# Second cross-attention of a two-layer decoder: a step's stages in another order, and the maxima of two heads turned together

## The chip, the cores and the metric

The kernel runs on one core of a Trainium2 chip, in float32. The metric is the device time of one execution in microseconds. Four runs of the kernel before gave 878.8 to 882.66, with a median of 880.27.

## The reference

A decoder of two layers works on `x` (8 sequences of 128 tokens, 256 wide) and a context `ctx_2048` of the same shape. Each layer is self-attention, cross-attention and a feed-forward part, each added to its input and followed by a layernorm. The last feed-forward part is a mixture of 64 experts with 8 chosen per token. The part that matters here is the cross-attention of the second layer; query is `x`, key and value are the context, both taken "as they lie" and cut into heads by reshaping:

```python
b, d, m = q.shape                  # 8, 128, 256
qh = q.reshape(b * h, d // h, m)   # h = 8 heads of 16 rows
kh = k.reshape(b * h, d // h, -1)
vh = v.reshape(b * h, c // h, -1)
qk = jnp.einsum('bdm,bdn->bmn', qh, kh) * scale
sm = jax.nn.softmax(qk, axis=-1)
ret = jnp.einsum('bmn,bcn->bcm', sm, vh)
```

A head is thus 16 of the 128 token rows, and its attention runs over the 256 columns. After it comes `x = _layernorm(x + ret)`, and then the routing of the experts: logits `x @ gate_w.T`, their softmax, the top 8 of 64.

## The kernel before

The parts of the decoder follow each other; within a part, work is cut into units and run as a pipeline written in Python and fully unrolled. On PE the order of instructions is the order in which the program issues them (`manual_schedule` for the tensor engine). On DVE, ACT and POOL a planner fixes the order when the kernel is built, by its own costs and by when it takes an operand to be ready; the program's order is its priority among ready instructions. The planner also gives out the buffers.

The second cross-attention works on 16 units (b, par): sequence b, and par 0 or 1 for one of the two heads in each block of 32 rows. So a unit has four heads, in row blocks j = 0 to 3 at rows 32j. It runs in these stages:

- `limits` (L803) copies the query on POOL with only the rows of this par kept (L806), and computes scores for maxima on PE (L812): four matmuls of 32 rows into four PSUM tiles `y_s`, each 128 query columns by 2 x 256 keys, both pars at once, for the half c = par of the query columns. Then DVE takes the four maxima, negated (L820, "maxima").
- `shift` (L824) turns the maxima on PE (L827, two transposes into one PSUM tile `y_m`), so that each lands in a spare row beside its head's query rows, and adds the query on DVE (L829). A row of ones in the keys then subtracts the maximum within the scores' matmul.
- `weights` (L832) computes transposed scores (L836, four PSUM tiles `y_sT`), and ACT their exponentials (L843, "y_e").
- `weigh` (L848) multiplies by the values and by ones for the sums (L855). For par 1 it ends the sequence: a reciprocal and a product on DVE (L862, L864), an addition on POOL (L866, on DVE for the last sequence), and a layernorm over DVE and POOL (L181 to L192).
- `turn_x`, `choose` and `place` (L869, L887, L912) do the routing for two sequences at a time (one at a time for the last two): a DMA of the rows to memory (L876) and transposes on PE (L880), the gate's matmuls and the top 8 on DVE (L894 to L909), then the places within the experts (L924 to L930) and the softmax (L944 to L951).

The pool `ps_x` has six PSUM buffers of one bank. From it come the tiles of `limits` (four), of `weights` (four), of `shift` (one) and of the routing (one each). The two sums of `weigh` lie in another pool of two.

`run_pipelined` (L44) runs one unit further at each step; within a step it goes through the stages from the deepest to the first, so that a step before issues: `place` of unit s-8, `choose` s-7, `turn_x` s-6, `weigh` s-4, `weights` s-3, `shift` s-2, `limits` s. After each of the first three steps `finish_heads` (L957) issues a sequence of the self-attention's output projection. There are 24 steps, 0 to 23; the last `limits` is in step 15, the last `weigh` in step 19.

Of the kernel before, what the change touches and what calls it, by code (L numbers as in the profile page):

```python
# [9 lines left out]
F32 = mybir.dt.float32  # L10
# [4 lines left out]
ALU = mybir.AluOpType  # L15
AX = mybir.AxisListType

P = 128
B = 8
# [24 lines left out]
def run_pipelined(units, stages, between=lambda step: None):  # L44

    states = [{} for _ in units]
    for step in range(len(units) + len(stages) - 1):
        for depth in range(len(stages) - 1, -1, -1):
            n = step - depth
            if 0 <= n < len(units):  # L50
                stages[depth](states[n], *units[n])
        between(step)
# [7 lines left out]
def decoder_kernel(ctx: ExitStack, tc: tile.TileContext, i, out):  # L60
    nc = tc.nc
# [33 lines left out]
    ident = cp.tile([P, P], F32, name="ident")  # L95
# [14 lines left out]
    rows_of, quarter = [], []  # L110
    for par in range(2):
        m = cp.tile([P, 1], F32, name=f"rows_{par}")
# [3 lines left out]
        q = cp.tile([P, 1], F32, name=f"quarter_{par}")  # L116
# [5 lines left out]
    def load(name, shape, src, dtype=F32, pool=cp):  # L122
        t = pool.tile(shape, dtype, name=name)
        nc.sync.dma_start(out=t, in_=src)
        return t
# [7 lines left out]
    for h in range(HALVES):  # L133
        t = xtp.tile([P, 2, HT], F32, tag="xT", name=f"xT0_{h}")
# [6 lines left out]
    for p in range(PAIRS):  # L141
        t = xsp.tile([P, 2, D], F32, tag="xs", name=f"x0_{p}")
# [19 lines left out]
    cx = load("cx", [P, B, D], i["ctx"].rearrange("b s d -> s b d"))  # L162
# [319 lines left out]
    with l0, tc.tile_pool(name="l0a", bufs=2) as ap:  # L482
# [33 lines left out]
        held = {}  # L516
# [139 lines left out]
    keys = kpool.tile([P, B, 2, D], F32, name="keys")  # L656
# [3 lines left out]
    one_row = []  # L660
    for par in range(2):
        m = cp.tile([P, 1], F32, name=f"one_row_{par}")
        nc.vector.reduce_sum(m, one_at[:, 1 - par, 0, :], axis=AX.X)
        one_row.append(m)
        t = cp.tile([P, 1], F32, name=f"kept_{par}")
# [3 lines left out]
    def make_constants():  # L669

        nc.gpsimd.memset(before, 1.0)
        nc.gpsimd.affine_select(
            before, before, pattern=[[1, P]], compare_op=ALU.is_gt, fill=0.0, base=0, channel_multiplier=-1
        )
        nc.gpsimd.iota(iota, pattern=[[1, P]], base=0, channel_multiplier=0, allow_small_or_imprecise_dtypes=True)
        nc.gpsimd.iota(starts, pattern=[[P, P]], base=0, channel_multiplier=0, allow_small_or_imprecise_dtypes=True)
        nc.gpsimd.iota(
            numbers, pattern=[[S, B]], base=0, channel_multiplier=1, allow_small_or_imprecise_dtypes=True
        )
        nc.gpsimd.tensor_scalar(numbers, numbers, 1.0 / (B * S), 1.0, ALU.mult, ALU.add)  # L680
        nc.gpsimd.iota(turns, pattern=[[1, TOP]], base=0, channel_multiplier=0, allow_small_or_imprecise_dtypes=True)
        nc.gpsimd.iota(rows_16, pattern=[[1, P], [0, TOP]], base=0, channel_multiplier=0, allow_small_or_imprecise_dtypes=True)
        nc.gpsimd.tensor_scalar(rows_16, rows_16, -MIDDLE, None, ALU.add)
        nc.gpsimd.iota(blks_16, pattern=[[1, NG], [0, TOP]], base=0, channel_multiplier=0, allow_small_or_imprecise_dtypes=True)
        nc.gpsimd.memset(seen[:, 0, :], 0.0)
        for par in range(2):
            nc.gpsimd.tensor_scalar(keys[:, :, par, :], cx, quarter[par], one_row[par], ALU.mult, ALU.add)

# [81 lines left out]
    def ps_x(name):  # L772
        return psx.tile([P, 512], F32, tag="x", name=name)

    with (
# [6 lines left out]
        cxT = load("cxT", [P, 2, B, S], i["ctxT"].rearrange("(k p) b c -> p k b c", p=P), pool=ap)  # L782
        values, sums_w, maxima = [], [], []
        for n in range(2):
            t = ap.tile([P, 2, 2, P], F32, name=f"maxima_{n}")
            nc.gpsimd.memset(t.rearrange("p a c r -> p (a c r)"), 0.0)
            maxima.append(t)
        for par in range(2):
            t = ap.tile([P, 2 * B, 4, 2, 16], F32, name=f"values_{par}")
            nc.gpsimd.memset(t.rearrange("p a j two r -> p (a j two r)"), 0.0)  # L790
            nc.gpsimd.tensor_copy(
                t[:, :, :, par, :],
                cxT.rearrange("p k b (j two r) -> p (k b) j two r", two=2, r=16)[:, :, :, par, :],
            )
            values.append(t.rearrange("p (k b) j two r -> p k b (j two r)", k=2))
            t = ap.tile([P, 2, 16], F32, name=f"sums_w_{par}")
            nc.gpsimd.memset(t[:, 1 - par, :], 0.0)
            nc.gpsimd.memset(t[:, par, :], 1.0)
            sums_w.append(t.rearrange("p two r -> p (two r)"))
        def rows_at(j):  # L800
            return slice(32 * j, 32 * j + 32)

        def limits(st, b, par):  # L803

            q = xp.tile([P, D], F32, tag=f"qm{par}", bufs=3, name=f"y_qm_{b}_{par}")
            nc.gpsimd.tensor_scalar(q, x4[b // 2][:, b % 2, :], kept[par], None, ALU.mult)  # L806
            st["q"] = q

            c = par
            tiles = [ps_x(f"y_s_{b}_{c}_{j}").rearrange("p (par n) -> p par n", par=2) for j in range(4)]  # L810
            for j in range(4):
                nc.tensor.matmul(  # L812
                    tiles[j], x4[b // 2][rows_at(j), b % 2, c * P : (c + 1) * P], keys[rows_at(j), b],
                    start=True, stop=True,
                )
            flat = maxima[b % 2].rearrange("p par c r -> p (par c r)")
            for j in range(4):

                at = c * P + 32 * j + 16
                nc.vector.tensor_reduce(  # L820
                    flat[:, at : at + 2 * P - 15 : 2 * P - 16], tiles[j], AX.X, ALU.max, negate=True
                )

        def shift(st, b, par):  # L824
            pt = ps_x(f"y_m_{b}_{par}")[:, : 2 * P]
            for c in range(2):
                nc.tensor.transpose(pt[:, c * P : (c + 1) * P], maxima[b % 2][:, par, c, :], ident)  # L827
            t = xp.tile([P, D], F32, tag=f"qs{par}", name=f"y_q_{b}_{par}")
            nc.vector.tensor_tensor(t, pt, st["q"], ALU.add)  # L829
            st["q"] = t  # L830

        def weights(st, b, par):  # L832
            tiles = [ps_x(f"y_sT_{b}_{par}_{j}").rearrange("p (k m) -> p k m", k=2) for j in range(4)]
            for k in range(2):
                for j in range(4):
                    nc.tensor.matmul(  # L836
                        tiles[j][:, k, :], keys[rows_at(j), b, par, k * P : (k + 1) * P], st["q"][rows_at(j), :],
                        start=True, stop=True,
                    )
            st["e"] = []  # L840
            for j in range(4):
                e = xp.tile([P, 2, D], F32, tag="ye", bufs=8, name=f"y_e_{b}_{par}_{j}")
                nc.scalar.activation(e, tiles[j], AF.Exp)  # L843
                st["e"].append(e)

        held = {}

        def weigh(st, b, par):  # L848
            if par == 0:
# [18 lines left out]

        def turn_x(st, b, par):  # L869

            st["seqs"] = {(1, 1): (0, 2), (3, 1): (2, 2), (5, 1): (4, 2), (7, 0): (6, 1), (7, 1): (7, 1)}.get((b, par))
            if st["seqs"] is None:
                return
            b0, n = st["seqs"]
            x = x5[b0 // 2][:, b0 % 2 : b0 % 2 + n, :]
            nc.sync.dma_start(out=xd[b0 * S : (b0 + n) * S, :].rearrange("(b s) d -> s b d", s=S), in_=x)  # L876
            pt = ps_x(f"pt_moe_{b0}")[:, : 2 * n * S].rearrange("p (k t) -> p k t", k=2)
            for k in range(2):
                for bb in range(n):
                    nc.tensor.transpose(  # L880
                        pt[:, k, bb * S : (bb + 1) * S], x[:, bb, k * P : (k + 1) * P], ident
                    )
            t = xp.tile([P, 2, 2 * S], F32, tag="xT_moe", name=f"xT_moe_{b0}")
            nc.scalar.copy(t[:, :, : n * S], pt)
            st["xT"] = t
# [71 lines left out]
        def finish_heads(step):  # L957

            b = B // 2 + 1 + step
            if b < B:  # L960
                add_heads(b, 0, L1_HEADS)
                if b == B - 1:
                    l1v.close()

        run_pipelined(
            [(b, par) for b in range(B) for par in range(2)],
            [limits, idle, shift, weights, weigh, idle, turn_x, choose, place],
            finish_heads,
        )

    keys_pool.close()
    open_banks()
# [250 lines left out]
    for b in range(B):  # L1223
# [8 lines left out]
        r = tp.tile([P, D], F32, tag="r", bufs=4, name=f"moe_r_{b}")  # L1232
        nc.vector.tensor_tensor(r, ps, acc, ALU.add)
        st = sm.tile([P, 6], F32, tag="ln_st", name=f"st_l1f_{b}")
# [5 lines left out]
        shift = sm.tile([P, 1], F32, tag="ln_shift", name=f"shift_l1f_{b}")  # L1240
# [66 lines left out]
```

## Time and profile before

| what | value |
|---|---|
| median of four runs | 880.27 us |
| the profiled execution | 880.5 us, span of the trace 878.6 us |
| scores for maxima, first to last start (L812) | 466.3 to 580.2 us |
| transposed scores (L836), first to last start | 492.7 to 595.1 us |
| end of the last `weigh` on PE | 600.1 us |
| routing and the first gathers | to 631 us |
| experts and output | to 878.6 us |
| PE busy over the span | 806.3 us (92%) |
| DVE, ACT, POOL busy | 460.3, 287.9, 231.7 us |
| DVE busy from 510.06 to 522.25 | 8.84 of 12.19 us |
| ACT busy in the same stretch | 4.13 us |

The span is the time from the first to the last instruction in the trace of one execution. A row of the timeline gives the start and the length of a group of like instructions, the engine, the line, what is written from what, their number, and in brackets the idle time before it with what ended it. PE rows are matmuls; PEld rows are the loading of a matmul's weights, which overlaps them. In the table of windows a row gives a stretch of time, its length, the busy time of PE, PEld, DVE, ACT and POOL (with the number of instructions), the clock granted to PE as a share of full speed, the share of the DMA engines and their GB/s.

### The profile page before, as it was taken

The numbers are of one execution on the slowest core, as the hardware profiler recorded it, in microseconds if no ns is written. First come the engines' busy times: TensorE is split into PE (matmuls) and PEld (weight loads), VectorE is DVE, ScalarE is ACT, GpSimd is POOL, SyncE is SP. The second block draws the span as 40 slices with busy tenths as digits, with TensorE's granted clock in tenths as the row PEclk, the third lists the DMA queues.
The fourth block names the chain that finished last, engine by engine and source line by source line (L and its number), as shares of the span: only waits on it lengthen the run. The fifth ranks groups of instructions, "written<-read, shape, count | busy, mean of one in ns | idle before, by whom it ended". The sixth has DMA issues, their size and how long they took to land. (4 is left out here: it accounts for less than half of the span.)

```text
span 878.6 us, 14286 instructions
## 1 busy us (share of the span) xinstructions
PE 806.3 (92%) x4588; PEld 541.1 (62%) x4588; DVE 460.3 (52%) x1280; ACT 287.9 (33%) x990; POOL 231.7 (26%) x321
## 2 busy tenths in 40 slices
PE   8899988999999999999999999995689888999946
PEld 5455643666455558555557655553578878888835
DVE  2799885314544432344444576756795333343326
ACT  2577751221333330233340132332332332333302
POOL 0011122216100001000014131111566655555524
PEclk9999996999999999999999998987599999999969
DMA  5400011920000000000010000000678887988665
GB/s 184 141 1 1 2 49 49 309 74 1 0 1 0 1 1 1 0 1 1 1 43 6 1 14 1 13 13 13 210 228 284 284 279 235 299 288 293 208 238 232
DMA packets 39730, 87.80 MB, mean 100 GB/s; under 512 B 6432, under 2 KB 16192, under 8 KB 38752
## 3 DMA queue, kind: packets, MB, share of 16 engines
q1 hardware_dynamic: 32352, 68.96, 23.8%
q0 software_dynamic: 6144, 16.79, 5.6%
q10 hardware_dynamic: 1152, 1.05, 0.4%
q8 instruction: 41, 0.67, 0.3%
q14 instruction: 41, 0.34, 0.1%
HBM read 76.29 MB, written 10.49 MB: 99 GB/s over the span
## 5 line engine op out<-in xcount | busy, mean ns | idle before, releaser
L224 ACT ACTIVATE l_e<-l_s,nm_l 128x128 f32<-128x128 f32 x256 | 90.2, 369 | 91.6 <-DVE nm_l L221 91.2
L1142 PE MATMUL moe_gu_few<-cols,w_few 128*128 (+1 forms) x832 | 114.9, 282 | 4.8 <-DVE cols L1121 1.9
L1142 PEld LDWEIGHTS moe_gu_few<-cols,w_few 128*128 128x128 f32 x832 | 103.0, 195 | 11.7 <-issue 8.9
L1172 POOL DMA_INDIRECT pair_rows<-moe_os_few,pairs x64 | 63.1, 986 | 54.0 <-DVE moe_os_few L1171 37.8
L1096 POOL DMA_INDIRECT xg_few<-x_rows,tok_i x60 | 62.0, 1034 | 32.2 <-PE moe_gu_few L1142 12.9
L1159 PE MATMUL moe_o_few<-moe_h_few,w_few 128*128 128x128 f32 x416 | 63.9, 277 | 0.0
L740 PE MATMUL l_q<-xT_l1a,w_qkv 128*128 128x512 f32 x128 | 60.2, 593 | 0.0
L843 ACT ACTIVATE y_e<-y_sT 128x512 f32<-128x512 f32 x64 | 33.0, 604 | 83.0 <-PE y_sT L836 50.3
L740 PE MATMUL l_v<-xT_l1a,w_qkv 128*128 128x512 f32 x128 | 60.1, 592 | 0.0
L740 PE MATMUL l_k<-xT_l1a,w_qkv 128*128 128x512 f32 x128 | 60.1, 592 | 0.0
L1162 ACT COPY cols<-moe_o_few 128x256 f32 (+1 forms) x104 | 38.8, 373 | 62.7 <-PE moe_oT_few L1169 22.3
L231 DVE TENSOR_SCALAR l_e<-l_e,inv_l 128x128 f32<-128x128 f32 x256 | 58.3, 292 | 1.4
L723 DVE TENSOR_TENSOR l_vs<-l_c,l_vs 128x512 f32<-128x512 f32 x32 | 22.1, 692 | 67.4 <-PE l_c L722 67.4
L703 PE MATMUL l_y<-w_o,l_vs 128*128 128x256 f32 x256 | 56.9, 381 | 0.0
L1159 PEld LDWEIGHTS moe_o_few<-moe_h_few,w_few 128*128 128x128 f32 x416 | 55.2, 193 | 0.0
L703 PEld LDWEIGHTS l_y<-w_o,l_vs 128*128 128x128 f32 x256 | 48.1, 190 | 9.9 <-issue 2.8
L1150 ACT ACTIVATE moe_s_few<-moe_gu_few 128x128 f32<-128x128 f32 x104 | 29.0, 279 | 76.3 <-PE moe_gu_few L1142 45.9
L224 ACT ACTIVATION_READ_ACCUMULATOR l_e<-l_s,nm_l 128x1 f32 x256 | 53.1, 207 | 0.0
L1121 DVE COPY cols<-moe_xT_few 128x256 f32<-128x256 f32 x64 | 26.5, 418 | 47.0 <-PE moe_o_few L1159 22.7
L1152 DVE TENSOR_TENSOR moe_h_few<-moe_gu_few,moe_s_few 128x128 f32<-128x128 f32 x104 | 29.8, 287 | 40.2 <-ACT moe_s_few L1150 25.5
L221 DVE TENSOR_REDUCE nm_l<-l_s 128x4 f32<-128x512 f32 x64 | 43.2, 685 | 10.0 <-PE l_s L755 8.1
L748 ACT COPY l_vs<-l_v 128x512 f32<-128x512 f32 x32 | 18.7, 585 | 78.6 <-PE l_v L740 78.6
(267 smaller groups left out, 1360.7 us busy)
## 6 DMA issues: line engine op xcount, KB each, us to landing
w_few<-in_experts SPq DMA_DIRECT2D x104, 384.0 KB
z<-pair_rows SPq DMA_DIRECT2D x7, 1024.0 KB
w_qkv<-in_w_qkv SPq DMA_DIRECT2D x8, 768.0 KB
w_o<-in_w_o SPq DMA_DIRECT2D x1, 2048.0 KB
xT<-in_xT SPq DMA_DIRECT2D x2, 512.0 KB
x<-in_x SPq DMA_DIRECT2D x4, 256.0 KB
cx<-in_ctx SPq DMA_DIRECT2D x1, 1024.0 KB
q_up<-in_up_qT SPq DMA_DIRECT2D x4, 256.0 KB
```

Source lines behind the costliest of these rows:

```text
L221: nc.vector.tensor_reduce(nm, s, AX.X, ALU.max, negate=True)
L224: nc.scalar.activation(e[:, a, :], s[:, a, :], AF.Exp, bias=nm[:, a : a + 1], scale=1.0, accum_out=sums[:, a : a + 1],)
L231: nc.vector.tensor_scalar(e[:, a, :], e[:, a, :], inv[:, a : a + 1], None, ALU.mult)
L703: nc.tensor.matmul(py[:, :D], scaled[b // 4, m][:, b % 4 * S : (b % 4 + 1) * S], w_o[:, m, :], start=(m == 0), stop=(m == L1_HEADS - 1),)
L740: nc.tensor.matmul(ps, w_qkv[:, k, c, n, :], xT[h][:, k, :], start=(k == 0), stop=(k == 1))
L843: nc.scalar.activation(e, tiles[j], AF.Exp)
L1096: nc.gpsimd.indirect_dma_start(out=x, out_offset=None, in_=xd, in_offset=bass.IndirectOffsetOnAxis(ap=tok_i[:, g : g + 1], axis=0), bounds ...
L1142: mm = nc.tensor.matmul(ps[:, a, :], ws[v][:, at : at + P], cols[:, k, bass.ds(o + P, P)], start=(k == 0), stop=(k == 1),)
L1152: nc.vector.tensor_tensor(hid, ps[:, 1, :], s, ALU.mult)
L1159: nc.tensor.matmul(ps[:, c, :], ws[v][:, at : at + P], hs[v], start=True, stop=True)
L1162: cp = nc.scalar.copy(cols[:, :, bass.ds(o, P)], ps)
L1172: inst = nc.gpsimd.indirect_dma_start(out=zd, out_offset=bass.IndirectOffsetOnAxis(ap=pairs[:, g : g + 1], axis=0), in_=o, in_offset=None, ...
```

## The change

Three things change together.

The order within a step is written out: `weights`, `weigh`, `place`, `choose`, `turn_x`, `shift`, `limits`, at the same depths 3, 4, 8, 7, 6, 2, 0 as before, in the same 24 steps.

The maxima of both pars are kept in one tile of half the width, with the place for a par 0 head's maximum at 32j + 16 of its block and for a par 1 head's at 32j. `shift` turns this tile once for a sequence, at par 0, and holds the PSUM tile for par 1. The DVE instruction now multiplies the turned tile by a mask of one row per block (`one_row`) and adds the query, so that each par sees its own maximum alone. The halves of the keys change places so that this fits.

The routing of the first three pairs of sequences starts at units (2, 0), (4, 0) and (6, 0) and so one step later; that of the last two sequences is unchanged.

```diff
-            nc.gpsimd.tensor_scalar(keys[:, :, par, :], cx, quarter[par], one_row[par], ALU.mult, ALU.add)
+            nc.gpsimd.tensor_scalar(keys[:, :, 1 - par, :], cx, quarter[par], one_row[par], ALU.mult, ALU.add)
...
-            t = ap.tile([P, 2, 2, P], F32, name=f"maxima_{n}")
+            t = ap.tile([P, 2, P], F32, name=f"maxima_{n}")
...
-                at = c * P + 32 * j + 16
-                nc.vector.tensor_reduce(
-                    flat[:, at : at + 2 * P - 15 : 2 * P - 16], tiles[j], AX.X, ALU.max, negate=True
-                )
+                at = c * P + 32 * j
+                nc.vector.tensor_reduce(flat[:, at : at + 17 : 16], tiles[j], AX.X, ALU.max, negate=True)
...
         def shift(st, b, par):
-            pt = ps_x(f"y_m_{b}_{par}")[:, : 2 * P]
-            for c in range(2):
-                nc.tensor.transpose(pt[:, c * P : (c + 1) * P], maxima[b % 2][:, par, c, :], ident)
+
+            if par == 0:
+                held[b, "m"] = ps_x(f"y_m_{b}")[:, : 2 * P]
+                for c in range(2):
+                    nc.tensor.transpose(held[b, "m"][:, c * P : (c + 1) * P], maxima[b % 2][:, c, :], ident)
             t = xp.tile([P, D], F32, tag=f"qs{par}", name=f"y_q_{b}_{par}")
-            nc.vector.tensor_tensor(t, pt, st["q"], ALU.add)
+            nc.vector.scalar_tensor_tensor(t, held[b, "m"], one_row[par], st["q"], ALU.mult, ALU.add)
...
-                        tiles[j][:, k, :], keys[rows_at(j), b, par, k * P : (k + 1) * P], st["q"][rows_at(j), :],
+                        tiles[j][:, k, :], keys[rows_at(j), b, 1 - par, k * P : (k + 1) * P], st["q"][rows_at(j), :],
...
-            st["seqs"] = {(1, 1): (0, 2), (3, 1): (2, 2), (5, 1): (4, 2), (7, 0): (6, 1), (7, 1): (7, 1)}.get((b, par))
+            st["seqs"] = {(2, 0): (0, 2), (4, 0): (2, 2), (6, 0): (4, 2), (7, 0): (6, 1), (7, 1): (7, 1)}.get((b, par))
...
-        run_pipelined(
-            [(b, par) for b in range(B) for par in range(2)],
-            [limits, idle, shift, weights, weigh, idle, turn_x, choose, place],
-            finish_heads,
-        )
+        units = [(b, par) for b in range(B) for par in range(2)]
+        states = [{} for _ in units]
+        stages = [(weights, 3), (weigh, 4), (place, 8), (choose, 7), (turn_x, 6), (shift, 2), (limits, 0)]
+        for step in range(len(units) + 8):
+            for stage, depth in stages:
+                if 0 <= step - depth < len(units):
+                    stage(states[step - depth], *units[step - depth])
+            finish_heads(step)
```

More of the change, by code (lines that the diff above doesn't have):

```diff
@@ L784, in decoder_kernel @@
         for n in range(2):
-            t = ap.tile([P, 2, 2, P], F32, name=f"maxima_{n}")
-            nc.gpsimd.memset(t.rearrange("p a c r -> p (a c r)"), 0.0)
+            t = ap.tile([P, 2, P], F32, name=f"maxima_{n}")
+            nc.gpsimd.memset(t.rearrange("p c r -> p (c r)"), 0.0)
             maxima.append(t)
@@ L799, in decoder_kernel @@
             sums_w.append(t.rearrange("p two r -> p (two r)"))
+        held = {}
         def rows_at(j):
@@ L815, in limits @@
                 )
-            flat = maxima[b % 2].rearrange("p par c r -> p (par c r)")
+            flat = maxima[b % 2].rearrange("p c r -> p (c r)")
             for j in range(4):
-                at = c * P + 32 * j + 16
-                nc.vector.tensor_reduce(
-                    flat[:, at : at + 2 * P - 15 : 2 * P - 16], tiles[j], AX.X, ALU.max, negate=True
-                )
+                at = c * P + 32 * j
+                nc.vector.tensor_reduce(flat[:, at : at + 17 : 16], tiles[j], AX.X, ALU.max, negate=True)
         def shift(st, b, par):
-            pt = ps_x(f"y_m_{b}_{par}")[:, : 2 * P]
-            for c in range(2):
-                nc.tensor.transpose(pt[:, c * P : (c + 1) * P], maxima[b % 2][:, par, c, :], ident)
+            if par == 0:
+                held[b, "m"] = ps_x(f"y_m_{b}")[:, : 2 * P]
+                for c in range(2):
+                    nc.tensor.transpose(held[b, "m"][:, c * P : (c + 1) * P], maxima[b % 2][:, c, :], ident)
             t = xp.tile([P, D], F32, tag=f"qs{par}", name=f"y_q_{b}_{par}")
-            nc.vector.tensor_tensor(t, pt, st["q"], ALU.add)
+            nc.vector.scalar_tensor_tensor(t, held[b, "m"], one_row[par], st["q"], ALU.mult, ALU.add)
             st["q"] = t
@@ L844, in weights @@
                 st["e"].append(e)
-        held = {}
         def weigh(st, b, par):
```

## The prediction

> **What bounds the kernel now.** I read the page first, then the PE timeline of the second cross-attention, then DVE's, then a table of windows for the clock. The page's second part has slices of 22 us; the changed step fills slices 21 to 27.
>
> ```profile
> PE   8899988999999999999999999995689888999946
> PEclk9999996999999999999999998987599999999969
> ```
>
> PE is above 90% busy there, and its granted clock dips in slices 24 and 26. So the step is PE's, but "busy" hides waits inside a group: a group's length against its shortest one shows them. One pair of steps in PE's timeline (start, length, line; the PEld rows are weight loads, with the wait in brackets):
>
> ```profile
> 516.48 1.15 PE L836 MATMUL y_sT<-y_q,keys 32*128 32x256 f32 x16
> 517.92 2.53 PE L812 MATMUL y_s<-keys,x 32*128 32x512 f32 x8
> 518.84 0.29 PEld L812 LDWEIGHTS y_s<-keys,x 32*128 32x128 f32 x2 [0.20 <-ACT y_e L843]
> 519.33 0.29 PEld L812 LDWEIGHTS y_s<-keys,x 32*128 32x128 f32 x2 [0.20 <-ACT y_e L843]
> 522.25 2.21 PE L836 MATMUL y_sT<-y_q,keys 32*128 32x256 f32 x16
> 523.33 0.72 PEld L836 LDWEIGHTS y_sT<-y_q,keys 32*128 32x128 f32 x10 [0.30 <-DVE maxima L820]
> 524.78 2.10 PE L812 MATMUL y_s<-keys,x 32*128 32x512 f32 x8
> ```
>
> The scores for maxima (L812) take 1.08 us where nothing holds them (484.57 to 485.65) and 2.1 to 2.5 here: their third and fourth tile wait for an exponential to give back a PSUM buffer. The scores (L836) take 1.08 alone and 2.1 where the maxima on DVE hold the buffers. Six buffers serve two groups of four, so whichever group comes right behind the other waits for the engine that empties the first. From 510.06 to 522.25 is 12.19 us for a pair of steps; PE's own work in it is 2 x (1.08 + 1.87 + 1.08 + 0.36) = 8.8. The weighing, 1.87 (514.62 to 516.48), lies between maxima scores and scores and covers DVE. DVE in those microseconds:
>
> ```profile
> 516.62 1.76 DVE L862 RECIPROCAL y_inv<-y_z 128x256 f32<-128x256 f32 x1 [0.39 <-PE y_z L855]
> 519.68 0.43 DVE L187 BATCH_NORM_STATS2 st_l1x<-y_r 128x6 f32<-128x256 f32 x1 [0.84 <-POOL y_r L866]
> 521.33 0.41 DVE L192 TENSOR_SCALAR x<-y_r,mv_l1x,rs_l1x 128x256 f32<-128x256 f32 x1 [1.00 <-POOL rs_l1x L182]
> 521.99 2.48 DVE L820 TENSOR_REDUCE maxima<-y_s 128x2 f32<-128x512 f32 x4
> ```
>
> Behind each second weighing stands a reciprocal and a layernorm, 5.1 us with two waits for POOL; the four maxima take 0.62 each. The clock, in windows cut at its own changes (behind each stretch its length, then busy time and instructions of PE, PEld, DVE, ACT and POOL, then the granted clock):
>
> ```profile
> 532.64:536.06 3.42, 3.42 (x43) 1.91 (x40) 2.38 (x7) 0.00 (x0) 1.73 (x3) 1.00 0.02 5
> 536.06:539.47 3.41, 2.56 (x23) 1.50 (x20) 3.17 (x15) 1.18 (x6) 0.00 (x0) 0.99 0.01 2
> 539.47:542.88 3.41, 3.41 (x10) 1.85 (x8) 2.50 (x7) 1.47 (x4) 0.92 (x1) 0.50 0.00 0
> 594.08:597.50 3.42, 2.67 (x25) 1.52 (x24) 2.78 (x16) 2.02 (x7) 0.00 (x0) 1.00 0.13 43
> ```
>
> A stretch of 3.41 us with 2.56 busy is followed by 6.8 us at half clock (twice, after 536 and 567, where the maxima scores wait for the routing's buffer); one with 2.67 is not.
>
> **The change, part by part.** I call a step odd where the weighing ends a sequence and the reciprocal follows. In the new order a step issues scores, weighing, (routing), turning, maxima scores. The exponentials now have the weighing as cover: scores end at 1.08, the fourth exponential about 1.2 + 2.06 = 3.3 us after their start (516.48 to 519.76), the maxima scores begin at 2.95 at the earliest and need their last buffer later: that wait goes. But maxima scores and the next scores are now neighbours, and what is late next is DVE.
>
> *Even step.* Weighing 1.87, turning 0.36, maxima scores. The first maximum starts 1.16 behind them (524.78 to 525.94); the scores' third tile needs the first, the fourth the second: 1.16 + 2 x 0.62 + 0.1 = 2.5, and 1.05 from the last release to the next group (523.33 to 524.38). 1.87 + 0.36 + 3.55 = 5.78. The turning used to lie in the exponentials' shadow and cost nothing; halved in number it now stands in the open.
>
> *Odd step.* DVE's order is fixed at build time, and the trace of before does not show it for this neighbourhood. Counted from the weighing's start: weighing to 1.87, reciprocal 2.01 to 3.77. With one maximum put between reciprocal and product, and one behind it: 4.39, product 4.81, second maximum 5.43, +0.1 + 1.05 = 6.58. Bounds: two maxima ahead of the product, 6.16; one behind the product and one behind the statistics, 7.45; all behind the layernorm (2.01 + 5.12 + 1.24 + 1.15), 9.5. I take 6.58, because of the tail of before:
>
> ```profile
> 600.13 1.76 DVE L862 RECIPROCAL y_inv<-y_z 128x256 f32<-128x256 f32 x1 [3.04 <-PE y_z L855]
> 601.81 0.17 DVE L901 MAX8 r_top<-gate 128x8 f32<-128x64 f32 x1
> 601.93 0.42 DVE L864 TENSOR_TENSOR y_r<-y_av,y_inv 128x256 f32<-128x256 f32 x1
> ```
>
> There a ready instruction was put between reciprocal and product. A pair is 12.36, against 12.19: an even trade.
>
> *Small edits.* The shift becomes a SCALAR_TENSOR_TENSOR; between its 0.29 (128x128, L930) and 0.69 (128x512, L935) lies 0.42 for 128x256, what L829 takes now. If the second shift were put late, the turned tile would hold a sixth buffer and the even steps wait for a third maximum: 6 x 0.62 = 3.7 more; zero taken. Smaller memsets and swapped halves of the keys on POOL: nothing, they lie under the first layer's heads. The three early DMAs of x rows go to SP's queue a step later; behind them there only the expert weights wait, first issued at 618.3.
>
> *Routing.* On PE the same 0.6 + 1.1 + 1.14 per block. But the top-8 choice now falls into odd steps (11 and 15): 1.8 + 0.65 us of DVE work (537.16 to 538.95 and the combine) join the reciprocal's; POOL's gaps take about 0.9, 1.5 remain on the path, twice 3.0. PE then idles some 1.5 us behind its first tile, so each keeps its clock loss. Price of one: between 2.2 (a routing block of four steps takes 30.3, two plain pairs and routing 27.2, less 0.85 idle) and 3.4 (half of 6.83); I take 2.8.
>
> *Plain odd steps.* Two tiles hold PE to about 3.8 (an estimate from the 1.05 that a tile's two halves take), the third starts at 4.5, the fourth at 5.53: 0.9 idle, 2.5 of 3.41 busy, under the 2.56 that cost the clock. The stretch from 3.8 to 5.53 lies whole in one window with a chance of (3.41 - 1.73)/3.41, about a half; of four plain odd steps two: 5.6.
>
> *Tail.* From the end of the scores of unit 13 to the last weighing's end: 585.18 to 600.03, 14.85, before, since each weighing waits for its exponentials. After: four weighings 7.48, two scores 2.16, placing 1.1, turning 0.36 and 0.7 for its shift, transposes 0.6: 12.4. Behind it, the choice of sequences 4 and 5 now falls into the last layernorm: 2.45 less DVE's 0.57 idle there, 1.9.
>
> *Sum.* The first scores start at 492.75 as before; those of unit 1 end at 498.0 (3.9 + 1.08 + 0.3). Six pairs 74.2, routing 4.5, choice 3.0, two clock losses 5.6: 585.3. Tail 12.4, choice 1.9: 599.6, against 600.03. Two more clock losses: +5.2. Routing, experts and output follow unchanged. The span of 878.6 belongs to a run of 880.5, the median is 880.27: **885.5**.
>
> **A page against the rows.** The Trainium skill, "TensorE: Matmul & The Clock Gate", section "Why this matters for your kernels", allows idle gaps up to about 3 us; by it the changed kernel would lose no clock and take 885.5 - 4 x 2.8 = 874.3. The rows differ: one gap of 0.85 us stands before 6.8 us at half clock. The same page's "A second HAM failure mode: psum-queue depth-cycling" speaks against this change: short idles between groups that cycle through PSUM buffers make the clock swing.
>
> **Rivals.** *No clock lost:* PE's idle pieces fall across windows, or DVE's order keeps PE above 2.6 busy of 3.41 in all six odd steps; the two old losses vanish too, and the tail's gain shows: 874.3, and 871.8 with odd steps of 6.16. For it: only 2.56 cost the clock, 2.67 did not. Against: the choice sits on the fullest step of DVE. *As many losses as now:* 879.9; the wait only changes its engine. For it: 12.36 against 12.19. *Layernorm first:* DVE's order keeps all maxima behind L192, as it stands from 516.62 to 521.99. Odd steps 9.5, 6 x 2.9 = 17.5 more: 903. For it: that very order; against: there the turned maxima came late on PE, here the tiles are ready before the reciprocal ends.
>
> **Chances.** Forecast 0.40 (879 to 892), no clock lost 0.24, as many losses 0.21, layernorm first 0.15. Half a per cent, 4.4 us, is about what a measurement tells from no change. Faster: the clock rival and a little of the next, 0.26; within: most of the third and the forecast's lower end, 0.27; slower 0.47. The range cuts the lower half of the clock rival and the upper half of the last: 872 to 901.
>
> **What will show it.** Maxima scores (L812's successor) at 1.1 us, not 2.5; scores at 2.4 in even and 3.6 in odd steps with DVE maxima as releaser; a maximum right behind the reciprocal; half clock after 3.41 us windows under 2.6 busy, four of them; the four last weighings at 1.87. I am wrong if the scores wait for nothing, or if the maxima stand behind the layernorm.

## The result, and the profile after

The changed kernel takes 883.95 us in the median (879.86 to 888.4), the kernel before 881.27 us in the same series: a ratio of 1.0029 with a 95% interval of 1.002 to 1.0038. It is slower by about 2.7 us, less than the half per cent called no change in the prediction. The profiled execution after took 884.19 us, with a span of 882.3 us; the one before had a span of 878.6 us.

The two rows of the page's second part for PE and its granted clock, after (slices of 22 us; the changed step fills slices 21 to 27):

```profile
PE   8999978999999999999999989886689888999856
PEclk9999996999999999999999988797599999999969
```

Counted from 0, slices 23, 24 and 25 now show the clock at 0.8, 0.8 and 0.7; before, 24 and 26 showed 0.8, with full speed between and ahead of them. What lies under them is in PE's timeline after, one odd step (start, length, engine, line, operation, count; idle time before the group and its releaser in brackets):

```profile
519.00 0.64 PE L855 MATMUL y_av<-y_e,values 128*32 128x256 f32 x8
...
520.86 1.14 PE L814 MATMUL y_s<-keys,x 32*128 32x512 f32 x8
521.82 0.60 PE L838 MATMUL y_sT<-y_q,keys 32*128 32x256 f32 x4
523.36 0.69 PE L838 MATMUL y_sT<-y_q,keys 32*128 32x256 f32 x2 [0.94 <-DVE maxima L822]
524.28 1.13 PE L838 MATMUL y_sT<-y_q,keys 32*128 32x256 f32 x10 [0.23 <-DVE maxima L822]
525.33 0.64 PE L855 MATMUL y_av<-y_e,values 128*32 128x256 f32 x8
```

The scores for maxima (L814) now run in 1.14 us without a wait, where they took 2.1 to 2.5; the scores (L838) behind them wait for two maxima instead. From weighing to weighing the odd step takes 525.33 - 519.00 = 6.33 us. DVE's timeline in the same step says why the maxima come when they do:

```profile
521.00 1.76 DVE L862 RECIPROCAL y_inv<-y_z 128x256 f32<-128x256 f32 x1 [1.92 <-PE y_z L855]
522.67 0.63 DVE L822 TENSOR_REDUCE maxima<-y_s 128x2 f32<-128x512 f32 x1
523.22 0.41 DVE L864 TENSOR_TENSOR y_r<-y_av,y_inv 128x256 f32<-128x256 f32 x1
523.54 0.68 DVE L822 TENSOR_REDUCE maxima<-y_s 128x2 f32<-128x512 f32 x1
524.46 0.43 DVE L187 BATCH_NORM_STATS2 st_l1x<-y_r 128x6 f32<-128x256 f32 x1 [0.24 <-POOL y_r L866]
524.81 0.68 DVE L822 TENSOR_REDUCE maxima<-y_s 128x2 f32<-128x512 f32 x1
```

The planner put one maximum on each side of the product, and the other two into the layernorm's gaps. The table of windows after, cut within 0.05 us of the clock's own changes (length, then busy time of PE, PEld, DVE, ACT and POOL, then the granted clock):

```profile
505.54:508.95 3.41, 2.24 (x22) 0.98 (x18) 3.23 (x4) 0.00 (x0) 0.59 (x1) 1.00 0.02 5
508.95:512.36 3.41, 3.41 (x26) 1.93 (x30) 2.09 (x5) 2.06 (x4) 0.92 (x3) 0.51 0.00 0
512.36:515.78 3.42, 3.42 (x30) 1.42 (x26) 0.58 (x2) 0.00 (x0) 0.00 (x0) 0.50 0.00 0
...
522.60:526.02 3.42, 2.44 (x27) 1.41 (x30) 3.18 (x8) 0.94 (x2) 0.99 (x3) 1.00 0.02 5
```

The wait of an odd step (0.94 + 0.23) leaves PE 2.24 busy of 3.41 and costs 6.8 us at half clock behind it; the same wait at 522.60 costs nothing (*The clock* below says why). There are five such stretches in the step, at 508.9, 536.3, 553.3, 570.4 and 587.5, of 6.8, 6.8, 6.8, 3.4 and 3.4 us: three of the four plain odd steps, and both steps with a top-8 choice. Before there were two of 6.8.

The time from the first scores to the end of the last weighing ("stage" in what follows) grew from 107.34 to 109.44 us; from there to the first matmul that lists the experts' tokens (`pair_in`, L1035 before, L1040 after) from 15.30 to 16.95; to the first matmul of the experts from 15.59 to 16.22; and the rest shrank from 247.62 to 246.76. The first scores start 0.18 later. Together that is 3.7 us more span.

### The profile page after: what moved, and what is told of

Read it like the earlier page. It is cut to its first block, busy times and chain, and to the rows that moved or that the text cites. A ratio compares the mean times of both kernels' runs of the same rounds, so it can differ in the third digit from the quotient of the medians.

```text
span 882.3 us, 14265 instructions
## 1 busy us (share of the span) xinstructions
PE 798.9 (91%) x4572; PEld 534.7 (61%) x4572; DVE 458.1 (52%) x1280; ACT 288.4 (33%) x990; POOL 231.2 (26%) x321
## 5 line engine op out<-in xcount | busy, mean ns | idle before, releaser
L838 PE MATMUL y_sT<-y_q,keys 32*128 32x256 f32 x256 | 40.8, 449 | 10.0 <-DVE maxima L822 8.8
```

Source lines behind the costliest of these rows:

```text
L838: nc.tensor.matmul(tiles[j][:, k, :], keys[rows_at(j), b, 1 - par, k * P : (k + 1) * P], st["q"][rows_at(j), :], start=True, stop=True,)
```

## The experiments

The experiments ran on chips where the kernel before takes 853.6 to 854.0 us. The 27 us or so that are missing lie almost all in the last part (experts and output: 218 to 223 us in all these profiles, against 247), not in the changed step, whose instructions have the same lengths. So each time is read as a ratio to the kernel before on its own chip, and parts of the step are compared within the stage. "Half clock" is the sum of the stretches in the stage in which the granted clock was 0.5.

| kernel | ratio, 95% interval | stage, us | half clock |
|---|---|---|---|
| before | 1 | 107.34 | 2 stretches, 13.7 us |
| after | 1.0029 [1.002, 1.0038] | 109.44 | 5, 27.3 |
| order_only | 1.0097 [1.0071, 1.0124] | 113.15 | 4, 23.9 |
| turn_only | 0.9984 [0.9965, 1.0003] | 103.62 | 2, 10.2 |
| route_early | 0.9955 [0.9931, 0.9979] | 102.01 | 3, 13.7 |
| fill | 0.9925 [0.99, 0.995] | 100.88 | 2, 6.8 |
| fill_early | 0.9935 [0.9911, 0.9959] | 97.02 | none |
| no_recip | 0.9978 [0.996, 0.9997] | 101.13 | 4, 17.1 |
| no_recip_before | 0.9845 [0.9827, 0.9864] | 95.63 | none |
| split_early | 0.998 [0.996, 1.0] | 103.64 | 3, 17.1 |
| evac_before | 0.999 [0.9966, 1.0015] | 107.43 | 2, 13.7 |
| turn_evac | 0.9954 [0.9928, 0.9979] | 103.07 | 2, 10.2 |
| early_evac | 0.9944 [0.9924, 0.9965] | 101.26 | 3, 13.7 |
| fill_evac | 0.9943 [0.9921, 0.9965] | 96.37 | none |

The stage and the half clock are those of one profiled execution each, the ratios those of 6 to 12 timed ones (51 for after): single executions of one kernel differ by some 8 us, so the stage is a reading and the ratio the result.

### The three parts of the change

**order_only**: the kernel before with only the new order of a step; the maxima are still turned for each unit, the routing starts at its old units.

```diff
-            [limits, idle, shift, weights, weigh, idle, turn_x, choose, place],
...
+        stages = [(weights, 3), (weigh, 4), (place, 8), (choose, 7), (turn_x, 6), (shift, 2), (limits, 0)]
...
```

> Kernel before with only the new order of a step; the maxima are turned once per unit and the routing starts at the old units. My account: the two engines' waits change places (pairs of 12.4 to 12.7 us against 12.2), eight more turnings of 0.36 stand in the open against the changed kernel (+2.9), the choice falls into even steps, where no reciprocal stands (-3.0): 884 us, within 3 of the changed kernel. Rival, that the turning together and not the order cost the time: 879 to 881, like the kernel before.

It came out at 1.0097, slower than either reading. Its PE timeline around two odd steps, and then DVE's in the second of them:

```profile
504.89 0.64 PE L855 MATMUL y_av<-y_e,values 128*32 128x256 f32 x8
...
512.80 0.93 PE L855 MATMUL y_av<-y_e,values 128*32 128x256 f32 x8
...
524.41 1.53 PE L836 MATMUL y_sT<-y_q,keys 32*128 32x256 f32 x6 [0.81 <-DVE y_q L829]
527.07 2.07 PE L836 MATMUL y_sT<-y_q,keys 32*128 32x256 f32 x10 [1.14 <-DVE maxima L820]
```

```profile
522.23 1.76 DVE L862 RECIPROCAL y_inv<-y_z 128x256 f32<-128x256 f32 x1 [1.92 <-PE y_z L855]
523.90 0.36 DVE L829 TENSOR_TENSOR y_q<-y_m,y_qm 128x256 f32<-128x256 f32 x1
...
524.51 0.68 DVE L820 TENSOR_REDUCE maxima<-y_s 128x2 f32<-128x512 f32 x1
526.00 0.43 DVE L187 BATCH_NORM_STATS2 st_l1x<-y_r 128x6 f32<-128x256 f32 x1 [0.81 <-POOL y_r L866]
526.34 0.67 DVE L820 TENSOR_REDUCE maxima<-y_s 128x2 f32<-128x512 f32 x1
```

In the new order a unit's shift stands directly ahead of its scores, with only the 1.08 us of maxima scores between. For par 1 that is the odd step: the addition (L829) stands behind the reciprocal, the scores wait 0.81 for it and then 1.14 for the second maximum. That one stands behind the layernorm's statistics here, which themselves wait 0.81 for POOL; in the changed kernel it stands ahead of them. The step takes 529.07 - 520.22 = 8.85 us, but its end lies at half clock; the odd step before it, at full clock, takes 512.80 - 504.89 = 7.91 instead of 6.33.

**turn_only**: the kernel before with only the maxima of both pars turned at once.

```diff
+            if par == 0:
+                held[b, "m"] = ps_x(f"y_m_{b}")[:, : 2 * P]
...
+            nc.vector.scalar_tensor_tensor(t, held[b, "m"], one_row[par], st["q"], ALU.mult, ALU.add)
```

> Kernel before with only the maxima of two heads turned at once; old order, old routing. My account: in the old order the turning lies in the exponentials' shadow, so halving it is worth nothing: 881, within 1.5 of the kernel before. Rival, that the 8 turnings saved come off PE's path: 8 x 0.36 = 2.9 less, 878.

0.9984, with 1 just inside the interval: in the old order the turning lay under the exponentials, and halving it brings nothing that can be told from no change.

**route_early**: the changed kernel with the routing at its old units, so order and turning without the later routing.

```diff
-            st["seqs"] = {(2, 0): (0, 2), (4, 0): (2, 2), (6, 0): (4, 2), (7, 0): (6, 1), (7, 1): (7, 1)}.get((b, par))
+            st["seqs"] = {(1, 1): (0, 2), (3, 1): (2, 2), (5, 1): (4, 2), (7, 0): (6, 1), (7, 1): (7, 1)}.get((b, par))
```

> Changed kernel with the routing's first three blocks at the old units, one step earlier, so that the choice falls into even steps. My account: the choice no longer joins the reciprocal on DVE: 3.0 us of path and one or two clock losses of 2.8 go: 876 to 881. Rival, that its place does not matter since PE waits for the maxima anyway: 884.

0.9955, as expected. So the later routing costs 1.0029 - 0.9955 = 0.74%, about 6.5 us. What the routing met, from DVE's timeline after, in the odd step from 546.88:

```profile
548.88 1.76 DVE L862 RECIPROCAL y_inv<-y_z 128x256 f32<-128x256 f32 x1 [1.92 <-PE y_z L855]
550.56 0.17 DVE L901 MAX8 r_top<-gate 128x8 f32<-128x64 f32 x1
...
554.11 0.69 DVE L822 TENSOR_REDUCE maxima<-y_s 128x2 f32<-128x512 f32 x1
```

Maximum, match and replacement of the top 8 stand between the reciprocal and the maxima, so that the third maximum starts at 554.11, 7.2 us after the weighing began, against 5.8 in the plain step above. In route_early the same choice falls into an even step, where DVE had been idle for 1.36 us ahead of it.

Order and turning do not add. Turning at once is worth 0.16% in the old order and 1.0097 - 0.9955 = 1.4% (12 us) in the new one; the stage says the same, 113.15 against 102.01 us.

### The clock

**fill**: the changed kernel, in which the scores of par 1 repeat their first two tiles' first halves twice: four more matmuls, into tiles that are written anyway, while PE would wait for the maxima.

```diff
-            for k in range(2):
-                for j in range(4):
+            for k, j in [(0, 0), (0, 1)] + [(0, 0), (0, 1)] * (2 * par) + [(0, 2), (0, 3)] + [(1, j) for j in range(4)]:
```

> Changed kernel that repeats the first two score matmuls of each par 1 unit twice (same tiles, same values), some 1.06 us of PE work in the idle time behind a reciprocal. My account: the plain odd steps (three half-clock stretches in the profile) keep the clock; each was worth 2.8: 876 to 878. Rival, that the lost clock is hidden because PE waits for DVE anyway: 884 to 886.

0.9925: against after 0.9925 / 1.0029 = 0.990, a little more than expected. PE's timeline of fill in an odd step that began at 518.46:

```profile
521.29 2.23 PE L837 MATMUL y_sT<-y_q,keys 32*128 32x256 f32 x14
523.75 1.13 PE L837 MATMUL y_sT<-y_q,keys 32*128 32x256 f32 x10 [0.23 <-DVE maxima L822]
524.80 0.64 PE L854 MATMUL y_av<-y_e,values 128*32 128x256 f32 x8
```

The step is no shorter: 524.80 - 518.46 = 6.34 us. Only the 0.94 us of idle time is gone. And with it the clock of the plain odd steps stays up; the row of the granted clock on fill's page has no dip in slices 23 to 27. The two stretches of 3.4 us that remain, in the steps with a choice (551.2 and 581.9), are too short to show there:

```profile
PEclk9999995999999999999999999999659999999969
```

So the idle pieces cost their time not by themselves but through the clock. 20.5 us less at half clock shorten the stage by 8.6, 0.42 for each; route_early against fill_early gives 5.0 for 13.7, 0.37.

What decides on a loss is not the busy share. Two windows of split_early (a kernel told of below) are equally busy. Behind the first the clock is halved, behind the second it is not:

```profile
536.10:539.52 3.42, 1.69 (x20) 1.07 (x24) 3.39 (x5) 2.06 (x4) 0.00 (x0) 1.00 0.01 2
553.17:556.58 3.41, 1.68 (x32) 0.75 (x25) 2.94 (x4) 2.07 (x4) 0.35 (x1) 1.00 0.00 0
```

The second holds 32 matmul instructions, the first 20. (A matmul of the program shows as two.) The traces allow a better count than either. An instruction of 512 columns takes 592 ns and one of 256 takes 379, so a column takes 0.83 ns. One that uses a quarter of the 128 x 128 array (32\*128 or 128\*32 in the rows) runs side by side with others: eight of 379 ns take 0.64 us together. So count for each instruction its columns, times 0.83 ns, times the share of the array it uses, and call the sum over a window its *array time*. An example is the window of the changed kernel from 505.57 on, ahead of its first loss:

```profile
505.51 1.14 PE L814 MATMUL y_s<-keys,x 32*128 32x512 f32 x8
506.47 0.60 PE L838 MATMUL y_sT<-y_q,keys 32*128 32x256 f32 x4
508.01 0.69 PE L838 MATMUL y_sT<-y_q,keys 32*128 32x256 f32 x2 [0.94 <-DVE maxima L822]
```

It holds 8 x 0.427 / 4 + 6 x 0.213 / 4 = 1.17 us. In each profile the stretches at half clock start whole multiples of 3.413 us apart. On that grid the fourteen profiles have 390 windows at full clock that start between 490 and 598 us. Behind 38 of them the clock fell. Of these, 37 have at most 1.25 us of array time and one has 1.31; of the 352 others none has less than 1.27. Some of them:

| kernel, start of the window | PE busy | array time | behind it |
|---|---|---|---|
| before, 536.0 | 2.56 | 1.16 | half clock |
| before, 594.0 | 2.67 | 1.44 | full clock |
| after, 505.6 | 2.25 | 1.17 | half clock |
| after, 522.6 | 2.47 | 1.32 | full clock |
| split_early, 536.1 | 1.69 | 0.99 | half clock |
| split_early, 553.2 | 1.68 | 1.34 | full clock |
| evac_before, 537.0 | 3.29 | 1.16 | half clock |
| no_recip, 529.0 | 2.74 | 1.24 | half clock |
| no_recip, 542.7 | 2.77 | 1.27 | full clock |
| route_early, 551.7 | 2.62 | 1.31 | half clock |

The bound was found by sorting these windows afterwards, and no kernel was built to test it. But it accounts for fill: its eight more instructions add 8 x 0.213 / 4 = 0.43 us to an odd step. No window over a plain odd step of fill has less than 1.53, and the two ahead of its losses have 0.75 and 1.14.

**fill_early**: fill with the routing at its old units (both diffs above).

> Changed kernel with both: the routing one step earlier, as in route_early, and the repeated score matmuls, as in fill. If the two gains are of different causes (1.3 per cent for the clock, 0.7 for the choice on DVE), they add: 0.986 of the kernel before (0.982 to 0.989). Rival, that both worked by the same lost clock: no better than fill, 0.992.

0.9935, the rival's number. Not one stretch at half clock is left in the stage, and it is 3.9 us shorter than fill's in the one profile, but the median doesn't show that: the two intervals overlap. The two profiles are no fair pair. Fill's execution has the lowest mean granted clock of its seven (0.949, median 0.955), fill_early's the highest of its eight (0.960, median 0.956). Why the early routing adds nothing to fill in the median stays open.

### The reciprocal

**no_recip** and **no_recip_before**: the changed kernel and the kernel before, with a copy in place of the reciprocal, 0.42 us on DVE instead of 1.76.

```diff
-            nc.vector.reciprocal(inv, pz[:, :D])
+            nc.vector.tensor_copy(inv, pz[:, :D])
```

> Changed kernel with a copy (0.42 us) in place of the reciprocal (1.76 us); it leaves the reciprocal out, so that the heads' sums are multiplied and not divided by. My account: the maxima behind it come 1.3 us earlier, odd steps lose their wait (about 0.9 us in each of six), and the half clock in the plain odd steps goes (three times 2.8): 0.985 of the kernel before. Rival, that the odd steps wait for the buffers whoever fills DVE: 1.000 to 1.003.

> Kernel before with the same copy in place of the reciprocal (same part left out). My account: there the weighing covers DVE, and only the wait of some 1.0 us in every second group of scores shortens, and the tail's last chain by 1.3: 0.990 to 0.995. If the reciprocal weighs as much here as in the changed kernel, the order has nothing to do with it: 0.985 or less.

Both missed, in opposite directions: 0.9978 and 0.9845. A shorter DVE helps the new order by 0.5% and the old one by 1.6%. (Without the reciprocal the values differ, and with them the choice of experts; but the experts and the output take 221.9 and 220.7 us in the two profiles, within the 218 to 223 of the others.) In the new order the odd step is 5.86 us long (514.88 to 520.74) and its scores still wait in two pieces (PE's timeline of no_recip):

```profile
518.65 0.69 PE L838 MATMUL y_sT<-y_q,keys 32*128 32x256 f32 x2 [0.35 <-DVE maxima L822]
519.68 1.12 PE L838 MATMUL y_sT<-y_q,keys 32*128 32x256 f32 x10 [0.34 <-DVE maxima L822]
```

Four losses of the clock remain. Two windows of no_recip, one ahead of a loss and one that cost nothing, stand close to the bound, at 1.24 and 1.27 us of array time:

```profile
529.04:532.45 3.41, 2.73 (x28) 1.31 (x24) 2.83 (x7) 0.32 (x1) 1.51 (x3) 1.00 0.00 0
532.45:535.86 3.41, 3.41 (x33) 1.37 (x32) 0.93 (x2) 1.75 (x4) 0.00 (x0) 0.50 0.03 7
...
542.69:546.10 3.41, 2.75 (x18) 1.41 (x16) 2.67 (x12) 0.00 (x0) 0.99 (x3) 1.00 0.00 0
```

In the old order the scores run at 1.15 us in both steps of the pair, the pair takes 11.53 us (511.37 to 522.90) instead of 12.19, and both losses are gone (PE's timeline of no_recip_before):

```profile
513.23 1.15 PE L836 MATMUL y_sT<-y_q,keys 32*128 32x256 f32 x16
514.31 0.44 PE L827 MATMUL y_m<-ident,maxima 128*128 128x128 f32 x2
514.68 2.53 PE L812 MATMUL y_s<-keys,x 32*128 32x512 f32 x8
```

The old order thus stood on DVE as well: what remains of its waits is the exponentials' (2.53), and the stage of this profile has no loss of the clock.

### Two tries to shorten it further

**split_early**: route_early with the weighing cut in two, its second half behind the maxima scores, so that work lies between them and the next scores.

```diff
-        stages = [(weights, 3), (weigh, 4), ... (shift, 2), (limits, 0)]
+        stages = [(weights, 3), (weigh_0, 4), ... (shift, 2), (limits, 0), (weigh_1, 4)]
```

> Changed kernel with the routing one step earlier and the weighing cut in two: half of it between scores and maxima scores, half between maxima scores and the next scores, so that both waits for buffers get 0.9 us of cover. My account: even steps 5.2 us instead of 5.8; in odd steps the reciprocal becomes ready behind the maxima, but the next weighing then waits for the reciprocal to give back its two sums: 0.980 to 0.992. Rival, that the wait for the sums eats all of it: 0.996 or more.

0.998, the rival's side, and not told from route_early's 0.9955 with certainty. The scores no longer wait, but the next weighing does (PE's timeline of split_early):

```profile
513.13 0.64 PE L854 MATMUL y_av<-y_e,values 128*32 128x256 f32 x8 [1.73 <-DVE y_inv L868]
```

The sums' pool has two buffers, one sequence's sums and products. The reciprocal now starts half a weighing later, and the next weighing, the first of another sequence, waits for it to give them back.

**evac_before**, **turn_evac**, **early_evac**, **fill_evac**: the kernel before, turn_only, route_early and fill_early, in which ACT copies the gate's logits out of PSUM at once, so that the routing no longer holds one of the six buffers until its exponentials.

```diff
+            logits = xp.tile([P, 2, NE], F32, tag="r_lg", name=f"r_lg_{b0}")[:, :n]
+            nc.scalar.copy(logits, ps)
+            ps = logits
```

> Kernel before, with the gate's logits copied by ACT into SBUF as soon as they are there, so that the routing gives its PSUM buffer back at once. If the two half-clock stretches of the kernel before come from the maxima scores' 0.85 us wait for that buffer, they go: two times 3.0 us, 0.992 to 0.994. Rival, that the reciprocal's lateness alone makes them: 1.000.

> Old order and old routing, both heads' maxima turned at once, logits copied out as in evac_before. Sum of the two: 0.998 x 0.993 = 0.991. Rival, no half clock was left to save: 0.998.

> New order, routing one step earlier, logits copied out. Here the next scores wait for the buffer behind a choice (3.4 us for fourteen of their matmuls): one or two of three half-clock stretches go, 0.988 to 0.993 against 0.9955 for route_early. Rival, that those scores wait for the maxima, which stand behind the top 8 on DVE: no change, 0.9955.

> The same with the repeated score matmuls. The profile of fill_early has no half clock left before the last weighing, so there is little to save: 0.990 to 0.9935. If it comes out under 0.988, the buffer and not the clock was the cost.

None of the four differs from its kernel without the copy by more than the intervals allow (0.999 against 1; 0.9954 against 0.9984; 0.9944 against 0.9955; 0.9943 against 0.9935). All four came out above what was expected. In evac_before the buffer is free, but the wait only changes its owner. ACT's timeline and then the weight loads' in the same step:

```profile
538.49 0.35 ACT L947 ACTIVATE r_e<-r_lg,nm_r 128x64 f32<-128x64 f32 x1 [3.49 <-DVE nm_r L943]
...
539.17 2.03 ACT L843 ACTIVATE y_e<-y_sT 128x512 f32<-128x512 f32 x4
```

```profile
539.79 0.29 PEld L812 LDWEIGHTS y_s<-keys,x 32*128 32x128 f32 x2 [0.95 <-ACT y_e L843]
```

The scores' exponentials stand on ACT behind the routing's, and those wait for the negated maximum of the logits, which DVE takes late. Both losses of the clock stay.

## Why the prediction was right

The forecast was 885.5 us from 880.27, 5.2 more; measured were 2.7 more in the median and 3.7 in the spans. Its mechanism held, and by its terms:

- **Maxima scores free of their wait**: 1.1 forecast, 1.14 measured in every plain step.
- **Even step**: 5.78 forecast, 5.80 measured (525.33 to 531.13).
- **Odd step**: 6.58 forecast from a maximum on each side of the product; DVE's order is that, the step 6.33. The excess is that the durations were added, while on DVE each instruction starts some 0.09 before the one ahead of it ends (522.67 against 521.00 + 1.76).
- **A pair** is 12.13 without a loss of the clock, 12.36 forecast, 12.19 before: the even trade. *Layernorm first* fell with the rows of DVE above.
- **Clock**: four losses forecast at 2.8 each, five seen. Against a pair of 12.13, and less what the routing adds, pairs with a loss are 3.2 (503.64 to 519.00), 3.0 and 1.5 longer, 2.6 in the mean: the price was about right. The count was one too low, and its reason holds: it depends on where the idle piece falls in a window. In the pair from 519.00 to 531.13, all at full clock, a window of 3.41 us has under 1.25 us of array time for 1.88 us of its possible starts, a chance of 0.55 against the half forecast; that three of the four fell and not two is luck. What does not hold is the measure, a busy share under 2.56: the array time decides.
- **Choice in odd steps**: 1.5 each and a loss of 2.8. The first such pair, from 546.88 to 564.75, is 17.87: 12.13, the gate's 1.1, the places' 0.55, and 4.1 for choice and loss together, against 4.3.
- **Scores of unit 13** end at 588.38; the sum gave 585.3 + 5.6 = 590.9.
- **Tail**: 12.4 forecast, 14.0 measured. Two things were missing: the last loss reaches to 590.9, into the first of the four weighings (3.1 instead of 1.87), and the weighing at 597.96 waits 0.81 for the reciprocal of the sequence before, as PE's timeline after has it; the 0.7 for the last shift is there (0.67).

```profile
593.07 1.15 PE L838 MATMUL y_sT<-y_q,keys 32*128 32x256 f32 x16 [0.67 <-DVE y_q L831]
...
597.96 0.64 PE L855 MATMUL y_av<-y_e,values 128*32 128x256 f32 x8 [0.81 <-DVE y_inv L862]
```

- **Behind the stage**: 1.9 forecast for the late choice, 1.65 measured; the rest (0.63 more, 0.86 less) is not explained by the change.

The scores of unit 13 end 2.5 us before the sum and the tail is 1.6 longer than in it. That these two misses partly cancel is luck, and so is part of the closeness of the total.

The *no clock lost* rival was given 874.3, 1.3% under the forecast. fill, which keeps the clock in the plain odd steps, lies 1.0% under after, some 9 us for three losses fewer, so 3 for each: the price was fair, and the condition is not met by the kernel as changed. (fill_early lies 0.9% under after, but it moves the routing too.)

Two more steps of the prediction do not hold, though they did not move its sum. It said that the weighing "covers DVE" in the old order: no_recip_before shows that DVE's reciprocal weighs 1.6% there. And it counted the turning at once only by its 0.36 us in the open; by order_only it is the condition under which the new order is not a loss of 1%. Taken apart, the change is order and turning together, a gain of 0.45% (route_early), and the later routing, a loss of 0.74%. Of the versions run that leave nothing out, fill is the fastest by its ratio, 0.9925 [0.99, 0.995], faster than both kernels; fill_early, fill_evac, early_evac and route_early overlap with it.

What stays open is how far the losses vary from one execution to the next. The spread of some 8 us fits such a variation: in every kernel of the experiments the longer executions tend to be those with the lower mean granted clock (correlations from -0.44 to -0.92). The record does not say where in the kernel that clock was lost.

## What to carry to other kernels

When two groups of tiles share a pool that is too small for both, turning their order round moves the wait to the other engine; read what that engine does in the same microseconds, and put nothing else of it (a reciprocal, a top-8 choice) into the step that is already its fullest. An idle piece of 0.9 us on PE can cost more through the clock than by itself: try harmless matmuls in it, which here brought 1.0% without making the step shorter. To see whether the clock is in danger, count the matmuls' columns times the share of the array they use, and not PE's busy row, which can stay full while quarter-array matmuls wait. And try the parts of a compound change one by one, because here one of them cost more than the other two gained, and two of them were only worth having together.

## What the runs showed of the hardware

- The clock granted to PE fell for 3.4 or 6.8 us at a time after idle pieces of 0.9 + 0.2 us in a step of 6.3 us. The Trainium skill, "TensorE: Matmul & The Clock Gate", section "Why this matters for your kernels", would let gaps up to about 3 us pass; the runs differ, since the longest idle time of PE in the stage after is 0.94 us and there are five losses. The same page's "A second HAM failure mode: psum-queue depth-cycling" agrees with the runs: there short idles between groups that cycle through PSUM make the clock swing, and here filling them removed three of five losses.
- On the clock's own grid of 3.413 us, all 37 windows of the stage with at most 1.25 us of array time were followed by half clock, and one of the 353 with more. Windows of 1.68 us of busy time stood on both sides, and one of 3.29 was followed by half clock.
- A microsecond at half clock lengthened the stage by 0.37 to 0.42 us in two pairs of single profiles, less than the 0.5 of a PE that does nothing but work. That PE waits for DVE and ACT in part of it anyway is the likely reason; no run isolates it.
- On DVE a reciprocal of 128x256 out of PSUM takes 1.76 us, a copy or a product of the same shape 0.42: the reciprocal is the one instruction behind which the whole step had to be arranged.
